# First-layer attention scores on tiles of the TensorE array, and half of the folded head weights on VectorE, in a graph-attention layer

## The chip, the cores and the metric

The kernel runs on one core of one Trainium2 (trn2) chip. The metric is device time of one execution in microseconds (us), as the median of the runs; every run also lists the granted clock of TensorE.

## The reference, cut to what matters

128 graphs of 64 nodes with 512 features pass through a layer norm and a ReLU, then a graph-attention layer with four heads, a second one with a single head, a feed-forward block, a second layer norm, and a residual addition. All is fp32.

```python
def _gat_heads(x, adj, W, a):
    Wh = einsum('bnf,hfo->bhno', x, W)
    f1 = einsum('bhno,ho->bhn', Wh, a[:, :O])
    f2 = einsum('bhno,ho->bhn', Wh, a[:, O:])
    e = f1[:, :, :, None] + f2[:, :, None, :]
    e = where(e > 0, e, 0.01 * e)
    e = where(adj > 0, e, NEG_INF)
    return einsum('bhnm,bhmo->bhno', softmax(e), Wh)

h   = relu(layernorm(x))                       # x: [128, 64, 512]
h   = elu(_gat_heads(h, adj, W_heads, a_heads)) # 4 heads of 512
out = elu(_gat_heads(h, adj, W_out, a_out))     # 1 head
ffn = relu(out @ w1 + b1) @ w2 + b2
x   = x + layernorm(ffn + out) * gamma + beta
```

## The kernel before

A tile holds 128 rows, which is two graphs. Four tiles make a group, so there are 16 groups.

**The scores.** f1 and f2 of the first layer come straight from the normalised input: the head weights W and the vectors a are folded once into `wa` (512 rows, 8 columns). f2 is needed along the free axis, so VectorE spreads it over a diagonal (`dg`) and TensorE multiplies by blocks of ones; f1 is added on VectorE.

```python
def project_f(p):                        # p: a pair of tiles
    pf = aux([P, 2, 2 * H], f"pf{p}")
    for j in range(2):
        hT = HT.pop(2 * p + j)
        for k in range(KC):
            nc.tensor.matmul(pf[:, j, :], hT[:, k, :], wa[:, k, :], ...)
    FF[p] = sm.tile([P, 2, 2, H], FP, ...)
    nc.vector.tensor_copy(FF[p], ...)
...
def softmax(f1, q, tag, t):
    dg = DG.pop(tag)
    pe = aux([P, q, N], f"{tag}pe{t}")
    nc.tensor.matmul(pe, blkones, dg, start=True, stop=True)
    nc.vector.tensor_tensor(e, pe, f1..., ALU.add)
    nc.vector.tensor_tensor(e, e, negm..., ALU.add)
    ...
```

**The products.** The large products are done in Strassen-Winograd form: seven products per matrix, one bank of PSUM each for products 1, 5 and 6; product 7 adds onto the bank of product 6 (`own[7] = 6`). VectorE must have read product 6 out (tile `t`) before product 7 may write there. With the order 1, 6, 5, 2, 7, 3, 4 it has the time of products 5 and 2 for that.

```python
own = {1: 1, 2: 1, 5: 5, 3: 5, 6: 6, 7: 6, 4: 6}
def after(p):
    if p in (1, 5, 6):
        nm = {1: "s1", 5: "s15", 6: "t"}[p]
        sb[nm] = wk.tile([P, 2, T], FP, tag=nm, ...)
        if p == 1:
            nc.scalar.copy(sb[nm], gb[1])
        else:
            nc.vector.tensor_tensor(sb[nm], gb[p], sb["s1"], ALU.add)
    ...
```

**The side list.** While TensorE does the steps of one large product, `run` asks for other work between them, evenly. Empty entries (`None`) only space the others out. Stage_a (scores and softmax of the group after next) has 15 entries; together with the feed-forward of the group before (`ff`), its transposes, the attention steps and the four finishing norms (`fin`) there are 45.

```python
def run(steps, side=()):
    side, done = list(side), 0
    for i, fn in enumerate(steps):
        fn()
        while done * len(steps) < (i + 1) * len(side):
            side[done]()
            done += 1

def stage_a(g):
    ...
    return [norms(p), norms(r), transposes(p), transposes(r),          # each a lambda
            f(p), None, attn_weights(p), f(r), None, attn_weights(r),
            None, transpose_weights(p), None, None, transpose_weights(r)]

# main loop, group g
tail = mix(ff, stage_a(g + 2))           # by place: (i + 0.5) / length
run(project2(g), mix(attn, tr) + tail + fin)
```

The next group's first products (tile `g_a`, `project1`) follow directly; beside them run `scores2`, eight multiply-accumulates on VectorE (tile `jf`).

## Time and profile before

| kernel before | value |
|---|---|
| median of 4 runs | 2445.72 us (2442.99 to 2447.22) |
| span of the profiled run | 2447.4 us |
| TensorE, VectorE, ScalarE, GpSimd busy | 97, 59, 31, 41% |
| period of one group | 144.96 us |

The prediction below shows the page's main lines. The list of waits of TensorE (us in total, times, longest) has for `g_a`:

```profile
PE g_a L240 <- issue: 5.3, 3, 3.2
```

One of the three, 1.45 us, is in the start. The other two stand before product 7, in the last two groups: 0.7 us and 3.2 us. In the last group VectorE's `t_a` ends only 10.1 us after the group's first product.

```profile
667.74 0.68 DVE L207 TENSOR_TENSOR t_a<-g_a,s_a 128x512 f32<-128x512 f32 x1
```

Four products take 670.80 - 663.90 = 6.90 us. The fifth in order, product 7, starts at once, because VectorE's `t_a` is over at 667.74 + 0.68 = 668.42, which is 4.5 us after the group's first product. TensorE needs it at 6.9 us, so the margin is 2.4 us.

### The profile page before, as it was taken

To read this page: it belongs to the slowest core of one execution; us is meant where nothing else is said; L and a number is where in the kernel's file an instruction comes from. 1 tells how busy PE (TensorE), PEld (TensorE's weight loads), DVE (VectorE), ACT (ScalarE), POOL (GpSimd) and SP (SyncE) were. 2 spreads that over 40 slices of the span, in tenths; PEclk is the share of its full clock that TensorE was granted. 3 is DMA by queue.
4 is the path that set the end of the run, shared out by engine and by line. 5 is a ranking of instruction groups with operands and counts; after the bars stand their busy time and mean duration, and the time that the engine had idled before them with its cause. 6 is when DMAs were issued, how large, how long until landed. Compare 5 with 4: busy or idle time off the path is not lost.

```text
span 2447.4 us, 32886 instructions
## 1 busy us (share of the span) xinstructions
PE 2382.2 (97%) x11745; PEld 2020.3 (83%) x11745; DVE 1446.5 (59%) x2515; ACT 770.9 (31%) x1353; POOL 1006.6 (41%) x848
## 2 busy tenths in 40 slices
PE   6799999999999999999999999999999999999996
PEld 6688888888888888888888888888888888878884
DVE  2655566474755748566574855657475574844536
ACT  1242514324152332414233251422415133231402
POOL 5733442534434344432534443253443435433323
PEclk6799999999999999999999999999999999999998
DMA  7644445454544545444454544545454454535442
GB/s 291 216 131 130 132 141 167 128 177 133 167 134 130 176 130 176 133 143 153 132 177 129 172 130 144 166 127 179 130 168 133 133 173 132 173 113 170 142 149 69
DMA packets 260481, 368.97 MB, mean 151 GB/s; under 512 B 22336, under 2 KB 145248, under 8 KB 260320
## 3 DMA queue, kind: packets, MB, share of 16 engines
q1 hardware_dynamic: 252160, 345.90, 44.2%
q10 hardware_dynamic: 5280, 10.49, 1.2%
q0 software_dynamic: 2880, 10.49, 1.1%
q8 instruction: 95, 1.56, 0.3%
q14 instruction: 66, 0.54, 0.1%
HBM read 339.53 MB, written 27.26 MB: 150 GB/s over the span
## 4 chain that ended last, share of the span: by engine, by line
PE 93%; DVE 3%; DMA 2%; issue 1%; POOL 1%; ACT 0%; SPq 0%; DVEq 0%; ACTq 0%; POOLq 0%
PE g_b L255 31%; PE g_a L240 31%; PE g_c L240 8%; PE g_d L255 7%; PE pz L453 4%; PE pf L314 2%; PE pa L585 2%; DMA x<-in_x_dram 1%; PE pzS L453 1%; PE pto L611 1%; PE s1pe L341 1%; PE pth L304 1%; PE s1pt L399 1%; PE pwa L147 1%; DVE o L658 0%
## 5 line engine op out<-in xcount | busy, mean ns | idle before, releaser
L255 PE MATMUL g_b<-w,h 128*128 128x256 f32 x2560 | 599.0, 380 | 0.0
L255 PEld LDWEIGHTS g_b<-w,h 128*128 128x128 f32 x2560 | 478.7, 190 | 74.6 <-issue 14.3
L240 PE MATMUL g_a<-zs_z,w 128*128 128x256 f32 x1536 | 357.9, 381 | 8.2 <-issue 5.3
L240 PE MATMUL g_a<-z,w 128*128 128x256 f32 x1536 | 363.0, 379 | 0.0
L240 PEld LDWEIGHTS g_a<-zs_z,w 128*128 128x128 f32 x1536 | 292.2, 191 | 57.3 <-issue 14.5
L240 PEld LDWEIGHTS g_a<-z,w 128*128 128x128 f32 x1536 | 291.6, 190 | 53.1 <-issue 15.2
L255 PE MATMUL g_b<-w,hS 128*128 128x256 f32 x1024 | 244.8, 385 | 0.0
L515 POOL TENSOR_TENSOR hS<-hS,h 128x512 f32<-128x512 f32 x64 | 81.4, 1272 | 385.0 <-DVE hS L477 384.4
L255 PEld LDWEIGHTS g_b<-w,hS 128*128 128x128 f32 x1024 | 189.5, 190 | 48.2 <-issue 13.0
L542 POOL TENSOR_TENSOR h<-h,h 128x512 f32<-128x512 f32 x64 | 84.2, 1315 | 286.0 <-PE g_b L255 285.9
L476 ACT ACTIVATE exc<-exc 128x512 f32<-128x512 f32 x256 | 161.0, 629 | 6.5
L265 POOL TENSOR_TENSOR zs_z<-zS,z 128x512 f32<-128x512 f32 x63 | 89.1, 1415 | 170.7 <-PE g_a L240 129.7
L477 DVE SCALAR_TENSOR_TENSOR h<-exc,h 128x512 f32<-128x512 f32 x128 | 104.5, 817 | 62.5 <-ACT exc L476 62.5
L542 POOL TENSOR_TENSOR h<-hS,h 128x512 f32<-128x512 f32 x64 | 81.3, 1271 | 138.6 <-PE g_b L255 138.5
L255 PE MATMUL g_d<-w,rt 128*128 128x256 f32 x512 | 122.2, 382 | 2.4 <-DVE n2ve L280 1.1
L267 POOL TENSOR_TENSOR zs_z<-z,zs_z 128x512 f32<-128x512 f32 x63 | 89.8, 1426 | 84.1 <-PE g_a L240 70.1
L475 ACT ACTIVATE exc<-h 128x512 f32<-128x512 f32 x128 | 80.6, 629 | 130.1 <-DVE h L512 130.1
L240 PE MATMUL g_c<-ot,w 128*128 128x256 f32 x512 | 121.0, 379 | 0.0
L240 PE MATMUL g_a<-zS,w 128*128 128x256 f32 x512 | 121.0, 379 | 0.0
L266 POOL TENSOR_TENSOR zs_z<-z,zs_z 128x512 f32<-128x512 f32 x63 | 80.6, 1280 | 80.5 <-PE g_d L255 63.7
L240 PEld LDWEIGHTS g_a<-zS,w 128*128 128x128 f32 x512 | 96.1, 190 | 18.8 <-issue 7.2
L255 PEld LDWEIGHTS g_d<-w,rt 128*128 128x128 f32 x512 | 96.0, 190 | 16.0 <-DVE n2ve L280 1.5
(145 smaller groups left out, 3754.9 us busy)
## 6 DMA issues: line engine op xcount, KB each, us to landing
w<-tc SPq DMA_DIRECT2D x640, 256.0 KB, 2.7
w<-in_L_gnn_W_heads_dram SPq DMA_DIRECT2D x192, 256.0 KB, 2.9
w<-in_L_gnn_W_out_dram SPq DMA_DIRECT2D x192, 256.0 KB, 2.8
w<-in_L_gnn_w_dram SPq DMA_DIRECT2D x96, 256.0 KB, 2.7
x<-in_x_dram SPq DMA_DIRECT2D x66, 256.0 KB, 4.0
xr<-in_x_dram SPq DMA_DIRECT2D x64, 256.0 KB, 2.8
out_dram<-o SPq DMA_DIRECT2D x64, 256.0 KB, 2.1
tc<-pt POOLq DMA_DIRECT2D x20, 512.0 KB, 4.8
```

The source lines that it names most:

```text
L240: nc.tensor.matmul(bk[:, o, :], w[:, k, ts(o, P)], a[:, k, :], start=start and o == 0 and k == 0, stop=k == 1, skip_group_check=True,)
L255: nc.tensor.matmul(bk[:, j, :], a[:, k, ts(j, P)], w[:, k, :], start=start and k == 0 and j == 0, stop=i == len(ms) - 1 and k == 1, skip_g ...
L265: eng.tensor_tensor(s2, s1, a11, ALU.subtract)
L266: eng.tensor_tensor(s4, a12, s2, ALU.subtract)
L267: eng.tensor_tensor(s3, a22, s2, ALU.subtract)
L314: nc.tensor.matmul(pf[:, j, :], hT[:, k, :], wa[:, k, :], start=(k == 0), stop=(k == KC - 1))
L453: nc.tensor.matmul(banks[b][:, c, :].rearrange("p (h n) -> p h n", h=H), src[rows, off + c * P:off + (c + 1) * P], at[rows, b], start=True ...
L475: nc.scalar.activation(ex, src, AF.Relu, scale=-1.0)
L476: nc.scalar.activation(ex, ex, AF.Exp, scale=-1.0)
L477: nc.vector.scalar_tensor_tensor(dst, ex, -1.0, src, ALU.add, ALU.max)
L515: nc.gpsimd.tensor_tensor(dst, dst, H1["22"][:, h], ALU.add)
L542: nc.gpsimd.tensor_tensor(dst[:, h], x0[:, h], x1[:, h], ALU.subtract)
```

## The change

The intent is to take 5.12 us per group of short TensorE work down by using parts of the array side by side, to start sooner, and to hide the last group's softmax.

- `project_f` computes f1 and f2 of four tiles transposed, with `wa` padded to 32 columns as the weight, on four column quarters of the array.
- The scores become a product of two factors: `L` holds f1 and ones, `R` holds ones and f2, and a sum over the small inner dimension gives f1 + f2. It runs on four quadrants.
- Two of the four heads are folded on VectorE, with no transposes on TensorE.
- The last group's softmax runs beside feed-forward steps.
- The weight ring shrinks from 12 to 11 buffers, and stage_a has another spacing.

```diff
-    ring = ctx.enter_context(tc.tile_pool(name="ring", bufs=12))
+    ring = ctx.enter_context(tc.tile_pool(name="ring", bufs=11))
...
-    wa = const.tile([P, KC, 2 * H], FP, name="wa")
+    wa = const.tile([P, KC, 32], FP, name="wa")
...
+    FH = 2
...
+    def fold_dve(m, ab):
+        for k in range(KC):
+            for c in range(2):
+                nc.vector.scalar_tensor_tensor(
+                    junk, MT[m][:, k, :], 1.0, ab[c], ALU.mult, ALU.mult,
+                    accum_out=wa[:, k, c * H + m:c * H + m + 1],
+                )
...
+    def project_f(g):
+        pf = aux([P, P], f"pf{g}")
+        for k in range(KC):
+            for j in range(G):
                 nc.tensor.matmul(
-                    pf[:, j, :], hT[:, k, :], wa[:, k, :], start=(k == 0), stop=(k == KC - 1)
+                    pf[32 * j:32 * j + 32], wa[:, k, :], HT[G * g + j][:, k, :],
+                    start=(k == 0), stop=(k == KC - 1), skip_group_check=True,
                 )
+        ...   # L: two ScalarE activations; U: VectorE; R: GpSimd (VectorE for group 0)
+    def scores1(g):
+        L, R = LR.pop(g)
+        pe = [aux([P, 2, H * N], f"s1pe{g}_{a}") for a in range(2)]
+        for q in range(2):
+            for a in range(2):
+                for b in range(NB):
+                    rows, cols = slice(64 * a, 64 * a + 64), slice(b * N, (b + 1) * N)
+                    nc.tensor.matmul(pe[a][cols, q, :]..., L[rows, q, cols], R[rows, :, cols], ...)
...
         return [
             lambda: norms(p), lambda: norms(r), lambda: transposes(p), lambda: transposes(r),
-            lambda: f(p), lambda: None, lambda: attn_weights(p), lambda: f(r), lambda: None,
-            lambda: attn_weights(r), lambda: None, lambda: transpose_weights(p), lambda: None,
-            lambda: None, lambda: transpose_weights(r),
-        ]
+        ] + wait + [lambda: project_f(g)] + wait * 2 + [
+            lambda: (scores1(g), attn_weights(p)), lambda: None, lambda: attn_weights(r),
+        ] + wait * 2 + [lambda: transpose_weights(p)] + wait * 2 + [lambda: transpose_weights(r)]
...
-            held = len(ff) - 7
-            run(project2(g), tr + [lambda: None] * 8 + ff[:held])
-            run(ff[held:] + fin, stage_e(g)[:15])
+            held = 2
+            run(project2(g), tr + [lambda: None] * 6 + ff[:held])
+            run(left, [scores2(g), ..., softmax2(g), ..., transpose_weights2(g), ..., attend2 x 4])
...
-    run(tr + ff[:12] + fin[:2] + ff[12:] + fin[2:])
+    run(tr + ff[:6] + last + ff[6:12] + fin[:2] + ff[12:] + fin[2:])
```

More of the change, by code (lines that the diff above doesn't have):

```diff
@@ L109, in gat_preln_kernel @@
     nc.vector.tensor_add(eye, ident[:, 0:N], ident[:, N:2 * N])
+    id32 = const.tile([P, 32], FP, name="id32")
+    nc.vector.tensor_reduce(id32, ident.rearrange("p (j r) -> p r j", r=32), AX.X, ALU.add)
+    headrow = const.tile([P, H], FP, name="headrow")
+    nc.vector.tensor_add(headrow, id32[:, 0:H], id32[:, H:2 * H])
+    isf = const.tile([P, 2], FP, name="isf")
+    nc.vector.tensor_reduce(isf, id32[:, 0:2 * H].rearrange("p (c h) -> p c h", c=2), AX.X, ALU.add)
+    isq = const.tile([P, 2, 2], FP, name="isq")
+    for q in range(2):
+        par = sm.tile([P, 1], FP, tag="par", name=f"par{q}")
+        nc.vector.tensor_reduce(
+            par, ident.rearrange("p (a q r) -> p q a r", a=2, q=2)[:, q], AX.XY, ALU.add
+        )
+        nc.vector.tensor_scalar(isq[:, q], isf, par, None, ALU.mult)
     mats = [W_heads[h] for h in range(H)]
@@ L117, in gat_preln_kernel @@
     MT, TC = {}, {}
-    wa = const.tile([P, KC, 2 * H], FP, name="wa")
+    wa = const.tile([P, KC, 32], FP, name="wa")
+    nc.vector.memset(wa, 0.0)
     def fetch(m):
@@ L122, in fetch @@
         nc.scalar.dma_start(out=MT[m], in_=mats[m].rearrange("(k p) o -> p k o", p=P))
+    FH = 2
     def load_a():
+        ar = wk.tile([2 * H, O], FP, tag="elu", name="ar", bufs=3)
+        nc.sync.dma_start(out=ar, in_=a_heads.rearrange("h (r p) -> (h r) p", p=O))
         rows = H * 2 * KC
@@ L128, in load_a, with spread_a, turn_a @@
         nc.sync.dma_start(out=ah, in_=a_heads.rearrange("h (r p) -> (h r) p", p=P))
+        return ar, ah
+    def spread_a(ar, m):
+        ab = []
+        for c in range(2):
+            pb = bank(f"pab{m}_{c}").rearrange("p a b -> p (a b)")
+            r = 2 * m + c
+            nc.tensor.matmul(
+                pb, ident[0:2 * H, r:r + 1].to_broadcast([2 * H, P]), ar, start=True, stop=True
+            )
+            ab.append(pb)
+        return ab
+    def turn_a(ah):
+        rows = H * 2 * KC
         pt = aux([P, rows], "pah")
@@ L131, in load_a, with fold_pe @@
         aT = const.tile([P, H, 2, KC], FP, name="aT")
-        nc.vector.tensor_copy(aT.rearrange("p h c o -> p (h c o)"), pt)
+        nc.scalar.copy(aT.rearrange("p h c o -> p (h c o)"), pt)
         return aT
-    def fold(m, aT, pw):
+    def fold_dve(m, ab):
+        for k in range(KC):
+            for c in range(2):
+                junk = wk.tile([P, O], FP, tag="t", name=f"jk{c}_{m}_{k}")
+                nc.vector.scalar_tensor_tensor(
+                    junk, MT[m][:, k, :], 1.0, ab[c], ALU.mult, ALU.mult,
+                    accum_out=wa[:, k, c * H + m:c * H + m + 1],
+                )
+    def fold_pe(m, aT, pw):
         for k in range(KC):
@@ L141, in fold @@
             wT = wk.tile([P, KC, P], FP, tag="elu", name=f"wT{m}_{k}", bufs=3)
-            if k % 2 == 0:
-                nc.scalar.copy(wT, pt)
-            else:
-                nc.vector.tensor_copy(wT, pt)
+            nc.scalar.copy(wT, pt)
             for o in range(KC):
                 nc.tensor.matmul(
-                    pw[:, k, :, m], wT[:, o, :], aT[:, m, :, o],
-                    start=(m == 0 and k == 0 and o == 0), stop=(o == KC - 1), skip_group_check=True,
+                    pw[:, k, :, m - FH], wT[:, o, :], aT[:, m, :, o],
+                    start=(m == FH and k == 0 and o == 0), stop=(o == KC - 1), skip_group_check=True,
                 )
@@ L295, in norm1 @@
             nc.gpsimd.tensor_tensor(HNS[t], HN[t][:, 0:T], HN[t][:, T:2 * T], ALU.add)
-    FF = {}
+    LR = {}
     HT = {}
@@ L306, in transpose_h @@
         nc.scalar.copy(HT[t], pt)
-    def project_f(p):
-        pf = aux([P, 2, 2 * H], f"pf{p}")
-        for j in range(2):
-            hT = HT.pop(2 * p + j)
-            for k in range(KC):
+    def project_f(g):
+        pf = aux([P, P], f"pf{g}")
+        for k in range(KC):
+            for j in range(G):
                 nc.tensor.matmul(
-                    pf[:, j, :], hT[:, k, :], wa[:, k, :], start=(k == 0), stop=(k == KC - 1)
-                )
-        FF[p] = sm.tile([P, 2, 2, H], FP, tag="f1", name=f"f1_{p}")
-        nc.vector.tensor_copy(FF[p], pf.rearrange("p t (c h) -> p c t h", c=2))
@@ L320, in gat_preln_kernel @@
-    DG = {}
-    def spread(f2, q, tag, t):
-        w = "s1" if q == 8 else "s2"
-        dg = sm.tile([P, q, N], FP, tag=w + "dg", name=f"{tag}dg{t}", bufs=1)
-        nc.vector.tensor_tensor(
-            dg,
-            eye[:, None, :].to_broadcast([P, q, N]),
-            f2[:, :, None].to_broadcast([P, q, N]),
+                    pf[32 * j:32 * j + 32], wa[:, k, :], HT[G * g + j][:, k, :],
+                    start=(k == 0), stop=(k == KC - 1), skip_group_check=True,
+                )
@@ new lines, in project_f @@
+        L = sm.tile([P, 2, P], FP, tag="L", name=f"L{g}", bufs=1)
+        for q in range(2):
+            nc.scalar.activation(L[:, q], pf, AF.Identity, bias=isq[:, q, 1:2], scale=isq[:, q, 0:1])
+        U = sm.tile([P, P], FP, tag="U", name=f"U{g}", bufs=1)
+        nc.vector.tensor_scalar(U, pf, isf[:, 1:2], isf[:, 0:1], ALU.mult, ALU.add)
+        R = sm.tile([P, H, P], FP, tag="R", name=f"R{g}", bufs=1)
+        eng = nc.vector if g == 0 else nc.gpsimd
+        eng.tensor_tensor(
+            R, U[:, None, :].to_broadcast([P, H, P]), headrow[:, :, None].to_broadcast([P, H, P]),
@@ L331, in spread @@
             ALU.mult,
         )
-        DG[tag] = dg
-    def softmax(f1, q, tag, t):
-        w = "s1" if q == 8 else "s2"
-        dg = DG.pop(tag)
-        pe = aux([P, q, N], f"{tag}pe{t}")
-        nc.tensor.matmul(
-            pe.rearrange("p h m -> p (h m)"), blkones.rearrange("p b n -> p (b n)"),
-            dg.rearrange("p h m -> p (h m)"), start=True, stop=True,
-        )
-        e = sm.tile([P, q, N], FP, tag=w + "e", name=f"{tag}e{t}", bufs=1)
-        nc.vector.tensor_tensor(e, pe, f1[:, :, None].to_broadcast([P, q, N]), ALU.add)
-        nc.vector.tensor_tensor(e, e, negm[:, None, :].to_broadcast([P, q, N]), ALU.add)
+        LR[g] = L, R
@@ new lines, in scores1 @@
+    def scores1(g):
+        L, R = LR.pop(g)
+        pe = [aux([P, 2, H * N], f"s1pe{g}_{a}") for a in range(2)]
+        for q in range(2):
+            for a in range(2):
+                for b in range(NB):
+                    rows, cols = slice(64 * a, 64 * a + 64), slice(b * N, (b + 1) * N)
+                    nc.tensor.matmul(
+                        pe[a][cols, q, :].rearrange("p (h m) -> p h m", h=H), L[rows, q, cols],
+                        R[rows, :, cols], start=(q == 0), stop=True, skip_group_check=True,
+                    )
+        for a in range(2):
+            E1[2 * g + a] = pe[a].rearrange("p t (h m) -> p (t h) m", m=N)
@@ L348, in softmax @@
+    def softmax(pe, f1, q, tag, t):
+        w = "s1" if q == 8 else "s2"
+        e = sm.tile([P, q, N], FP, tag=w + "e", name=f"{tag}e{t}", bufs=1)
+        mask = negm[:, None, :].to_broadcast([P, q, N])
+        if f1 is None:
+            nc.vector.tensor_tensor(e, pe, mask, ALU.add)
+        else:
+            nc.vector.tensor_tensor(e, pe, f1[:, :, None].to_broadcast([P, q, N]), ALU.add)
+            nc.vector.tensor_tensor(e, e, mask, ALU.add)
         nc.vector.scalar_tensor_tensor(e, e, ALPHA, e, ALU.mult, ALU.max)
@@ L380, in softmax @@
         return A
-    A1 = {}
-    def spread1(p):
-        spread(FF[p][:, 1].rearrange("p t h -> p (t h)"), 2 * H, "s1", p)
+    A1, E1 = {}, {}
     def attn_weights(p):
-        A1[p] = softmax(FF.pop(p)[:, 0].rearrange("p t h -> p (t h)"), 2 * H, "s1", p)
+        A1[p] = softmax(E1.pop(p), None, 2 * H, "s1", p)
     def transpose_weights(p):
@@ L422, in transposes @@
             transpose_h(2 * p + 1)
-        def f(p):
-            project_f(p)
-            spread1(p)
+        wait = [lambda: None]
         return [
             lambda: norms(p), lambda: norms(r), lambda: transposes(p), lambda: transposes(r),
-            lambda: f(p), lambda: None, lambda: attn_weights(p), lambda: f(r), lambda: None,
-            lambda: attn_weights(r), lambda: None, lambda: transpose_weights(p), lambda: None,
-            lambda: None, lambda: transpose_weights(r),
-        ]
+        ] + wait + [lambda: project_f(g)] + wait * 2 + [
+            lambda: (scores1(g), attn_weights(p)), lambda: None, lambda: attn_weights(r),
+        ] + wait * 2 + [lambda: transpose_weights(p)] + wait * 2 + [lambda: transpose_weights(r)]
     ZB = {}
@@ L568, in scores2 @@
                 )
-        F2[g] = f
-        spread(f[:, 1], G, "s2", g)
-    def softmax2(g):
-        A2[g] = softmax(F2.pop(g)[:, 0], G, "s2", g)
+        dg = sm.tile([P, G, N], FP, tag="s2dg", name=f"s2dg{g}", bufs=1)
+        nc.vector.tensor_tensor(
+            dg, eye[:, None, :].to_broadcast([P, G, N]), f[:, 1][:, :, None].to_broadcast([P, G, N]),
+            ALU.mult,
+        )
+        F2[g] = f, dg
+    def softmax2(g):
+        f, dg = F2.pop(g)
+        pe = aux([P, G, N], f"s2pe{g}")
+        nc.tensor.matmul(
+            pe.rearrange("p h m -> p (h m)"), blkones.rearrange("p b n -> p (b n)"),
+            dg.rearrange("p h m -> p (h m)"), start=True, stop=True,
+        )
+        A2[g] = softmax(pe, f[:, 0], G, "s2", g)
     def transpose_weights2(g):
@@ L586, in attend2 @@
         if j == 0:
-            OUT[g] = big.tile([P, G, FO], FP, tag="out", name=f"o{g}")
+            tag = "out" if g < NG - 1 else "z11"
+            OUT[g] = big.tile([P, G, FO], FP, tag=tag, name=f"o{g}")
         elu(OUT[g][:, j], pa, f"2_{g}_{j}")
@@ L671, in mix @@
         return [fn for _, _, fn in sorted(keyed, key=lambda k: k[:2])]
-    aT = load_a()
+    ar, ah = load_a()
     for m in range(H):
@@ L678, in gat_preln_kernel @@
         norm1(t)
+    ab = [spread_a(ar, m) for m in range(FH)]
+    aT = turn_a(ah)
     for t in range(G):
         transpose_h(t)
-    pw = aux([P, KC, 2, H], "pwa")
-    for m in range(H):
-        fold(m, aT, pw)
-    nc.vector.tensor_copy(wa.rearrange("p k (c h) -> p k c h", c=2), pw)
+    for m in range(FH):
+        fold_dve(m, ab[m])
+    pw = aux([P, KC, 2, H - FH], "pwa")
+    for m in range(FH, H):
+        fold_pe(m, aT, pw)
+    for c in range(2):
+        nc.vector.tensor_copy(wa[:, :, c * H + FH:(c + 1) * H], pw[:, :, c])
+    project_f(0)
+    scores1(0)
     for p in range(2):
-        project_f(p)
-        spread1(p)
         attn_weights(p)
@@ L731, in gat_preln_kernel @@
         else:
-            held = len(ff) - 7
-            run(project2(g), tr + [lambda: None] * 8 + ff[:held])
-            run(ff[held:] + fin, stage_e(g)[:15])
-    for fn in stage_e(NG - 1)[15:]:
-        fn()
+            held = 2
+            run(project2(g), tr + [lambda: None] * 6 + ff[:held])
+            left = ff[held:]
+            run(left, [
+                lambda: scores2(g), lambda: None, lambda: None, lambda: None, lambda: softmax2(g),
+                *[lambda: None] * 7, lambda: transpose_weights2(g), lambda: None,
+                *[lambda j=j: attend2(g, j) for j in range(G)], lambda: None,
+            ])
+    last = fin
     tr, ff, fin = feed_forward(NG - 1)
-    run(tr + ff[:12] + fin[:2] + ff[12:] + fin[2:])
+    run(tr + ff[:6] + last + ff[6:12] + fin[:2] + ff[12:] + fin[2:])
 _INS = [
```

## The prediction

> **What bounds the kernel now.** I read the page's list of engines first, then the 40 slices, then the chain that ended last.
>
> ```profile
> PE 2382.2 (97%) x11745; PEld 2020.3 (83%) x11745; DVE 1446.5 (59%) x2515; ACT 770.9 (31%) x1353; POOL 1006.6 (41%) x848
> PE   6799999999999999999999999999999999999996
> PEclk6799999999999999999999999999999999999998
> PE 93%; DVE 3%; DMA 2%; issue 1%; POOL 1%; ACT 0%; SPq 0%; DVEq 0%; ACTq 0%; POOLq 0%
> ```
>
> TensorE is busy for 97% of the span and carries 93% of the chain. Only the first two slices of 61 us and the last one show holes. So three places can give time: TensorE's own work in the middle, the start, and the end. Work on VectorE, ScalarE or GpSimd in the middle is hidden.
>
> Next the timeline of TensorE in the middle of one group of four tiles (columns: start us, us, engine, line, operation, tile, count).
>
> ```profile
> 574.96 1.89 PE L255 MATMUL g_b<-w,h 128*128 128x256 f32 x8
> 576.78 2.00 PE L453 MATMUL pz<-at,hn 64*128 64x256 f32 x16
> 578.71 1.99 PE L255 MATMUL g_b<-w,h 128*128 128x256 f32 x8
> ...
> 611.96 1.89 PE L255 MATMUL g_b<-w,h 128*128 128x256 f32 x8
> 613.69 1.85 PE L314 MATMUL pf<-wa,hT 128*128 128x8 f32 x16
> 615.39 1.97 PE L255 MATMUL g_b<-w,h 128*128 128x256 f32 x8
> ...
> 622.38 1.02 PE L341 MATMUL s1pe<-s1dg,blkones 128*128 128x512 f32 x2
> 623.24 1.89 PE L255 MATMUL g_b<-w,h 128*128 128x256 f32 x8
> ```
>
> I subtract starts, because the second column includes a pipeline tail that overlaps the next row. Eight g_b matmuls take 613.69 - 611.96 = 1.73 us, 0.216 us each for 256 columns. Sixteen pf matmuls of only 8 columns take 615.39 - 613.69 = 1.70 us, 0.106 us each: as much as 128 columns would, so the 128-column weight load (PEld) is what they pay for. Two s1pe matmuls of 512 columns take 0.86 us. Each occurs twice per group: 2 x 1.70 + 2 x 0.86 = **5.12 us per group**. In the source an fp32 product is one call; the trace counts two instructions for it (512 pf for 256 calls), and I count in those instructions.
>
> The same phase of g_a comes back every 144.95 us (starts 386.65, 531.61, 676.58), and no TensorE wait longer than a fraction of a microsecond lies in between. So a microsecond taken from TensorE there should be a microsecond saved, 15 times (the first group is in the start).
>
> The start, by stretches (per engine busy us and count; then PEclk, DMA share, GB/s), and two rows that fix its steps:
>
> ```profile
> 34.00:42.00 8.00, 6.00 (x30) 5.60 (x29) 1.88 (x3) 0.59 (x1) 5.65 (x7) 0.50 1.05 401
> 42.00:50.00 8.00, 8.00 (x41) 8.00 (x41) 1.70 (x3) 1.17 (x2) 5.48 (x7) 0.50 0.84 327
> 63.86 0.19 DVE L684 COPY wa<-pwa 128x32 f32<-128x32 f32 x1 [4.15 <-PE pwa L147]
> 100.71 1.99 PE L240 MATMUL g_a<-z,w 128*128 128x256 f32 x8
> ```
>
> The folded head weights (wa) are finished only at 63.9 us, at half the TensorE clock; the first Strassen product starts at 100.7 us.
>
> The end: the wait list gives TensorE 6.4 us before s2pt, waiting for VectorE's softmax of the last group.
>
> ```profile
> PE s2pt L579 <- DVE s2A L374: 6.4, 1, 6.4
> 2396.49 3.78 PE L585 MATMUL pa<-wh,at 128*128 128x512 f32 x4 [0.68 <-ACT at L581]
> ```
>
> After that idle stretch four pa take 3.78 us, some 0.86 us each, where the middle shows two in 0.86 us: the clock fell to half as well.
>
> **What the Trainium skill says.** (1) "TensorEngine Tiling (Array Packing)", Key Properties: tiles of the array load and multiply independently, but changing the tiling mode drains the engine. The trace agrees: sixteen pz, which use 64 rows each, take 578.71 - 576.78 = 1.93 us, against 16 x 0.216 = 3.46 us one after the other; half of 3.46 is 1.73, so two ran at once and about 0.20 us went to the switch. The g_b run behind it needs 1.83 us (to 580.54) instead of 1.73, another 0.10. I take **0.3 us per tiled run**. (2) "TensorE: Matmul & The Clock Gate", Part 3, gives 2.38 times for three column tiles and 10.6 for sixteen row-and-column tiles. No run so far shows column tiles, let alone in fp32; this is the step I am least sure of. (3) The same page, Part 1: an idle TensorE falls to half clock; the trace has 0.50 through the start and the slow pa at the end. (4) "VectorE: DVE Perf Modes" gives (N+151)/0.96 ns for an fp32 tensor operation, 691 ns at 512; the trace has 684 to 692 ns for such rows.
>
> **The change part by part.**
>
> *f1/f2 transposed (pf).* Removed: 32 instructions, 3.40 us per group. Added: 16 calls, 32 instructions of 128 moving columns, with wa padded to 32 columns as the weight, on four column quarters. One alone should take half of 0.216, so 0.108 us; all in a row 3.46 us; four at once 0.86 us. Plus 0.3 for the switch: 1.16 us. The weight load shrinks from 128 columns to 32 and should no longer bind.
>
> *Scores (s1pe).* Removed: 4 instructions of 512 columns, 1.72 us per group. Added: 8 calls, 16 instructions of 256 columns with 64 rows and 64 columns, on four quadrants: 16 x 0.216 = 3.46 in a row, 0.86 four at once, plus 0.3: 1.16 us. In the program the two instructions of one call are on the same tile, so four at once needs the engine to look past the waiting one. The pz pairs show that it does so for two tiles: otherwise half the calls would not have overlapped.
>
> So 5.12 becomes some 2.4 us with a little loss, 2.7 less, and 15 x 2.7 = **40 us**. If only two tiles overlap: 1.73 + 1.73 + 0.6 = 4.1, and 15 us. If none: 7.5, and 36 us lost.
>
> *Off the path in the middle.* VectorE loses 2 x (0.17 + 0.72 + 0.69) = 3.2 us per group (copy of f, s1dg, the f1 addition) and gains one 128-column operation; ScalarE gains two of 128 columns; GpSimd gains one 128x512 product (1.3 to 1.4 us in its rows). All three have room (busy 59, 31 and 41%). One weight buffer fewer (12 to 11) takes some 2 us of a lead of some 20 us; no TensorE wait for a weight DMA is listed. I give these nothing.
>
> *Start.* Half of the 16 fold steps leave TensorE. From 34 to 64 us the old kernel did 13 steps, 2.3 us each at half clock; eight less is 18 us. Against that, VectorE has 16 multiply-accumulates, about 0.75 + 0.08 us each by the jf rows (752 ns, and 79 ns for the accumulator read): 13.3 us, beside TensorE's 18. wa should be ready at about 46 us. The path behind it (products, scores, softmax, transposes) is a few us shorter too, but has a new chain of factor building. **20 us** in all.
>
> *End.* The last group's softmax now runs beside twelve of the feed-forward steps (1.73 us each, 21 us of TensorE work), so the 6.4 us wait and the half clock (eight pa x 0.43 = 3.4 us) should go. The normalisations of the group before move into the last feed-forward, where VectorE then has more to do (about 4 x 2.5 us). Net **8 us**.
>
> Sum: 40 + 20 + 8 = 68; 2445.4 - 68 = 2377. I say **2378 us**.
>
> **Rivals.** (a) Column quarters or quadrants do not overlap fully in fp32, because the moving streams or weight loads share a path. For: no column tile in the trace. Against: the pz pairs and the skill's figures. Two at once: 2378 + 25 = 2403. None: about 2445 to 2455, no gain. (b) A wait takes the place of the removed work: the scores now wait for a chain of three engines (ScalarE, VectorE, GpSimd) and GpSimd works in order, often held for g_b by write-after-read waits of 2 to 3 us. For: such waits stand in its timeline just at that point. Against: the new schedule leaves three steps, some 6 to 10 us, between projection and scores, where the chain needs about 0.35 + 0.3 + 1.4 us plus queueing. If it fails by 1 us per group: 2393. (c) The start is held by VectorE or by loads, not by the folds: with DMA share 1.0 until 42 us and VectorE waiting in order for x tiles, wa may come at 55 rather than 46: 2387.
>
> **Range and chances.** All right: 2365 to 2370. With (b) or (c) 2385 to 2395, with half of (a) 2400. Low 2352, high 2408. The 2% border is 2396.5, so the gain must exceed 49 us; the start and end alone (28 us) do not reach it. I put faster at 0.80, same at 0.17, slower at 0.03.
>
> **What would show each step.** Between rows of TensorE's timeline, the pf run should take about 1.2 us instead of 2 x 1.70, the scores run about 1.2 instead of 2 x 0.86; the period of g_a should fall from 144.95 to about 142.2 us with no new TensorE wait on R or L; wa should be written near 46 us and the first g_a start near 78; the wait before s2pt should be gone, and pa there should run at full clock. The prediction is wrong above all if tiles run one at a time.

## More of the kernel before

The timelines of TensorE and VectorE at a usual turn (start us, us, engine, line, operation, tile, shape, count):

```profile
663.90 1.89 PE L240 MATMUL g_a<-z,w 128*128 128x256 f32 x8
...
670.80 3.62 PE L240 MATMUL g_a<-zs_z,w 128*128 128x256 f32 x16
```

## The result, and the profile after

The changed kernel takes **2434.4 us** (median of 4 runs, 2432.96 to 2437.24) against 2445.72. The ratio of the two is 0.9956 with a 95% interval of 0.9939 to 0.9974, which at the 2% border is "same". Ratios here are the mean time of one kernel's fast runs over that of the other's of the same rounds, so they are not quite the ratio of the medians. The time lies 26 us above the predicted range.

The page's line of engines and TensorE's list of waits after the change:

```profile
PE 2344.2 (96%) x11849; PEld 1961.4 (81%) x11849; DVE 1451.6 (60%) x2468; ACT 787.1 (32%) x1386; POOL 1020.0 (42%) x863
```

```profile
PE g_a L284 <- issue: 31.5, 14, 3.5
...
PE s2pt L636 <- DVE s2A L427: 0.3, 1, 0.3
```

TensorE's busy time fell by 38.0 us where the span fell by only 14.6. `g_a` now waits before product 7 in 14 groups, 31.5 us in all. The wait before `s2pt` went from 6.4 to 0.3 us, as meant.

**The tiled runs.** TensorE's timeline around them:

```profile
458.48 1.08 PE L358 MATMUL pf<-hT,wa 128*32 128x128 f32 x32
459.50 1.99 PE L299 MATMUL g_b<-w,h 128*128 128x256 f32 x8
461.32 1.89 PE L284 MATMUL g_c<-zs_o,w 128*128 128x256 f32 x8
...
468.32 1.09 PE L383 MATMUL s1pe<-R,L 64*64 64x256 f32 x16
469.35 1.99 PE L299 MATMUL g_d<-w,rt 128*128 128x256 f32 x8
471.18 1.89 PE L299 MATMUL g_b<-w,hS 128*128 128x256 f32 x8
```

By differences of starts, `pf` takes 459.50 - 458.48 = 1.02 us and `s1pe` 1.03 us. The eight matmuls before and behind each of them take some 0.09 us longer than their usual 1.73 us. That is about 1.20 us for each run, 2.40 for both, where 5.12 stood before.

**The new wait.** The first products of the group's next turn, on TensorE and VectorE:

```profile
646.90 1.89 PE L284 MATMUL g_a<-z,w 128*128 128x256 f32 x8
...
652.08 1.89 PE L284 MATMUL g_a<-z,w 128*128 128x256 f32 x8
655.89 5.38 PE L284 MATMUL g_a<-zs_z,w 128*128 128x256 f32 x16 [1.93 <-issue]
661.11 1.89 PE L284 MATMUL g_a<-z,w 128*128 128x256 f32 x8
```

```profile
650.65 0.68 DVE L596 TENSOR_TENSOR wh<-g_b,s_b 128x512 f32<-128x512 f32 x1
...
655.11 0.68 DVE L251 TENSOR_TENSOR t_a<-g_a,s_a 128x512 f32<-128x512 f32 x1
```

Product 2 is issued from 652.08 and would be through at 652.08 + 1.73 = 653.81. Product 7 starts at 655.89, **2.1 us** late. The profile names no releaser ("issue"), but VectorE's `t_a`, which product 7 must wait for, ends at 655.79, 0.10 us before. The same 0.10 us stands in the other turns that I looked at (`t_a` over at 511.18, product 7 at 511.28; 802.13 and 802.24). `t_a` now ends 8.9 us after the group's first product instead of 4.5, and TensorE needs it at 6.9. Between the two VectorE rows stand four `jf`, one statistic of the next norm and `s2dg`, nearly without a gap: the chain is late as a whole.

The wait has a second cost. The sixteen matmuls behind it take 661.11 - 655.89 = 5.22 us instead of 3.45. Two stretches of 3.41 us (busy us and count of PE, PEld, DVE, ACT, POOL; then PEclk, DMA share, GB/s):

```profile
652.91:656.32 3.41, 1.49 (x7) 1.01 (x7) 3.38 (x12) 1.23 (x2) 0.00 (x0) 1.00 0.99 302
656.32:659.73 3.41, 3.41 (x10) 2.66 (x9) 2.44 (x6) 0.00 (x0) 0.34 (x1) 0.50 0.38 139
```

In the first VectorE is busy for 3.38 of 3.41 us, while TensorE, by its modelled ends, is busy for 1.49. In the second the granted clock is 0.50: 7 or 8 matmuls take about 0.43 us each. That happens behind 11 of the 14 waits and costs about 1.7 us each time.

Which waits it follows can be read from the trace. In this one, between 300 and 2300 us, the half clock always comes in single pieces of 3.41 us, and their starts are whole multiples of that length apart (803.09 - 656.32 = 146.77, which is 43 of them). I cut this part of the run into such windows and counted TensorE as idle from 0.216 us after its last start to its next one. Each of the 11 waits puts at least 2.09 us of idle TensorE into one window, and the next window has half clock. The other three lie across a border, with at most 1.87 us on either side (the one at 1092.76 to 1095.08 is 2.3 us long), and nothing follows. In the traces of e1, e2, e3, e7 and e8 the line falls at the same place, for waits over 1 us: 91 windows at full clock hold up to 1.98 us of them, and the clock stays full; 41 hold 1.99 us or more, and the next window has half clock.

**The accounts.** The chain of waits holds the same 72 `g_a` instructions of every group; the first and the last of them before and after (start us, us, engine, tile, line, count) split the span into start, middle and end:

```profile
241.20 15.54 PE g_a L240 x72
...
2271.05 15.54 PE g_a L240 x72
```

```profile
225.84 15.54 PE g_a L284 x72
...
2267.82 15.54 PE g_a L284 x72
```

| part | before, us | after, us | change, us | predicted, us |
|---|---|---|---|---|
| to the first of these | 241.20 | 225.84 | -15.4 | -20 |
| 14 periods between | 2029.85 | 2041.98 | **+12.1** | **-38** (14 x 2.7) |
| from the last on | 176.35 | 164.98 | -11.4 | -8 |
| span | 2447.4 | 2432.8 | -14.6 | |

The prediction's fifteenth 2.7 us falls outside these 14 periods. The miss is in the middle: a period mostly lasts 146.3 us where the half clock follows the wait, and 144.6 where it does not; before it lasted 144.96.

**The start.** On VectorE, GpSimd and TensorE:

```profile
48.16 0.24 DVE L747 COPY wa<-pwa 128x8 f32<-128x8 f32 x2 [12.68 <-PE pwa L191]
...
88.61 4.36 DVE L310 TENSOR_TENSOR zs_z<-z,zs_z 128x512 f32<-128x512 f32 x1
```

```profile
88.71 1.28 POOL L202 TENSOR_TENSOR pt<-pw 128x512 f32<-128x512 f32 x1
```

```profile
81.27 1.99 PE L284 MATMUL g_a<-z,w 128*128 128x256 f32 x8
...
98.20 3.78 PE L284 MATMUL g_a<-zs_z,w 128*128 128x256 f32 x8 [7.85 <-DVE t_a L251]
```

`wa` is there at 48.2 us instead of 63.9, and the first product at 81.3 instead of 100.7. But 7.85 us of that gain are then lost, again to `t_a`: a VectorE sum that takes about 0.7 us elsewhere takes 4.36 us beside three weight sums of GpSimd from 88.71 to 92.4, and `t_a` (97.45 to 98.14) stands behind it.

### The profile page after: what moved, and what is told of

It reads as the page before. It is cut to its first block, busy times and chain, and to the rows that moved or that the text cites. A ratio compares the mean times of both kernels' runs of the same rounds, so it can differ in the third digit from the quotient of the medians.

```text
span 2432.8 us, 33084 instructions
## 1 busy us (share of the span) xinstructions
PE 2344.2 (96%) x11849; PEld 1961.4 (81%) x11849; DVE 1451.6 (60%) x2468; ACT 787.1 (32%) x1386; POOL 1020.0 (42%) x863
## 4 chain that ended last, share of the span: by engine, by line
PE 92%; DVE 2%; issue 2%; POOL 2%; DMA 2%; ACT 0%; SPq 0%; DVEq 0%; POOLq 0%; ACTq 0%
PE g_b L299 32%; PE g_a L284 32%; PE g_c L284 8%; PE g_d L299 8%; PE pz L499 4%; PE pa L642 2%; PE pzS L499 1%; PE pto L669 1%; PE pth L348 1%; PE s1pt L449 1%; DMA pw<-in_L_gnn_W_out_dram 1%; PE s1pe L383 1%; PE pf L358 1%; DMA pw<-in_L_gnn_w_dram 0%; DMA aj<-in_adj_dram 0%
## 5 line engine op out<-in xcount | busy, mean ns | idle before, releaser
L284 PE MATMUL g_a<-zs_z,w 128*128 128x256 f32 x1536 | 376.7, 395 | 41.4 <-issue 31.5
L284 PEld LDWEIGHTS g_a<-zs_z,w 128*128 128x128 f32 x1536 | 304.0, 199 | 98.7 <-issue 43.9
```

What stands on the lines that cost most here:

```text
L284: nc.tensor.matmul(bk[:, o, :], w[:, k, ts(o, P)], a[:, k, :], start=start and o == 0 and k == 0, stop=k == 1, skip_group_check=True,)
```

## The experiments

My theory after the comparison: TensorE's saving is real; VectorE's chain at the end of a group is behind, and product 7 waits for its last member. At first I put that down to the later softmaxes (theory A); after e1 to e4, to the new spacing of the side work as a whole (theory A2). Rivals: the smaller weight ring; the place of the softmaxes; the new factors themselves; a start or an end that gives nothing. In the short diffs of stage_a the lambdas are left out. The runs were made on two chips (e5 to e8 on the second), each beside the kernel before on the same chip, with medians of 2443.69 to 2447.03 us. For a few us the difference of two ratios says more than that of two medians; each ratio is known to some 4 us.

| run | median us (lowest to highest) | ratio to before, 95% interval |
|---|---|---|
| e1 softmaxes earlier, 17 entries | 2480.22 (2475.97 to 2483.8) | 1.0144 (1.0124 to 1.0164) |
| e2 score sums moved | 2417.5 (2415.1 to 2420.66) | 0.9889 (0.9871 to 0.9907) |
| e3 kernel before, 17 entries | 2494.55 (2494.02 to 2495.81) | 1.0204 (1.0188 to 1.0221) |
| e4 kernel before, 11 buffers | 2444.85 | 1.001 (0.9983 to 1.0037) |
| e5 changed kernel, 15 entries | 2386.13 (2383.66 to 2386.3) | 0.975 (0.9735 to 0.9765) |
| e6 half of the score sums | 2386.93 | 0.9756 (0.9742 to 0.9771) |
| e7 old end | 2445.02 | 0.9997 (0.998 to 1.0014) |
| e8 old folding | 2444.59 | 0.9992 (0.9977 to 1.0007) |
| e9 filled wait | 2416.49 | 0.9881 (0.9862 to 0.99) |
| e10 e5 with later weight sums | 2382.4 (2381.41 to 2384.18) | 0.9746 (0.973 to 0.9761) |

### e1: the softmaxes earlier, the list as long

```diff
-        ] + wait + [project_f] + wait*2 + [(scores1, attn p), None, attn r]
-        + wait*2 + [tw p] + wait*2 + [tw r]
+        ] + [project_f] + wait + [(scores1, attn p), None, attn r]
+        + wait*2 + [tw p] + wait*3 + [tw r] + wait
```

> The changed kernel with one thing moved: in the side list of a group the joint projection stands one slot earlier and the scores with the first softmax two slots earlier (same length, same arithmetic). Theory A (VectorE is late: the joint projection pushed both softmaxes some 10 us later, into a stretch where VectorE has no room, so that t_a of head 0 comes about 2.1 us too late for the product that reuses its PSUM bank, and the clock then falls to half for seven matmuls): the wait shrinks to under 0.5 us in most groups, the slow matmuls go, the period of a group falls from 146.2 to about 142.5 us, the time to about 2385 us. Theory B (the wait is for weights, because of the 11 buffers, or for GpSimd's sums with its extra product R): nothing of theirs is moved, the wait stays near 2.1 us and the time near 2434 us.

It took 2480.22 us, 46 us more than the changed kernel, where theory A had expected some 50 less. The wait before product 7 was only a little shorter (1.6 to 1.7 us), and `t_a` still ended 8.4 us or more after the group's first product. A second wait came, 14 times and 43.2 us in all: TensorE's `g_d`, in the feed-forward, waited for `zs_r`, a block sum of VectorE.

```profile
633.11 3.36 PE L299 MATMUL g_d<-w,zs_r 128*128 128x256 f32 x8 [3.25 <-issue]
```

The run before it starts at 627.96, so 633.11 - 627.96 = 5.15 us pass for a run of 1.73; 3.4 us are lost, and the eight matmuls behind take 636.26 - 633.11 = 3.15 us, most of them at half clock. The place of the softmaxes alone is therefore not the cause of the first wait, and a step of side work moved on VectorE can make a wait elsewhere. The period was about 150.0 us.

### e2: the second layer's score sums moved

```diff
-            [scores2] + gap * 6 + [softmax2] + gap * 6
+            gap * 3 + [scores2] + gap * 5 + [softmax2] + gap * 4
```

> The changed kernel with the eight score sums of the second layer (jf, VectorE, 0.76 us each) emitted three slots later in the next group, so that t_a of head 0 can go before them on VectorE; nothing is taken away. Theory A: t_a comes 2 to 3 us sooner after the first products, the 2.1 us wait and the seven slow matmuls go, time about 2385 to 2395 us, unless the softmax of the second layer then comes late in its turn. Theory B: no change, about 2434 us.

It took 2417.5 us, 17 us less, but it did not test what it was meant to: the built program still had the `jf` ahead of `t_a` on VectorE. `t_a` ended at +8.6 to +8.8 us in most groups, and the wait was mostly 1.75 to 2.0 us. What changed is that the half clock mostly did not follow, as these waits leave less than 2 us of idle time in a window; the period was then 144.3 to 144.6 us. About the order of `jf` and `t_a` it is inconclusive.

### e3: only the spacing, in the kernel before

```diff
-            f(p), None, attn_weights(p), f(r), None, attn_weights(r), None, ...
+            None, None, f(p), None, attn_weights(p), f(r), None, attn_weights(r), None, ...
```

> The kernel before, whose arithmetic is untouched, with its two pairwise projections, scores and softmaxes delayed by two slots, to the slots where the changed kernel has its softmaxes. Theory A: the wait before the second product on the bank of t_a, and half-clock matmuls behind it, appear in the kernel before too; its period rises from 145.0 to 147 to 149 us and its time to 2475 to 2505 us. Theory B: no wait, period 145.0, time 2445 us as before.

Two empty entries, and no other change, made the kernel before some 2% slower: 2494.55 us (the interval of the ratio lies across the border of 2%). TensorE's and VectorE's timelines at the same place:

```profile
529.93 1.89 PE L240 MATMUL g_a<-z,w 128*128 128x256 f32 x8
533.75 3.48 PE L240 MATMUL g_a<-zs_z,w 128*128 128x256 f32 x15 [1.92 <-issue]
```

```profile
532.97 0.68 DVE L207 TENSOR_TENSOR t_a<-g_a,s_a 128x512 f32<-128x512 f32 x1
```

It is the wait of the changed kernel: `t_a` ends at 533.65, product 7 starts at 533.75, 2.1 us late. The list shows 33.0 us in 15 waits of `g_a`, 14 of them this one. The period is 147.5 us, or 149.3 to 149.6 where the half clock follows. The wait needs nothing of the new arithmetic. This run delays the softmaxes and lengthens the list at once, so it cannot tell the two apart; e1, with early softmaxes and a long list, does.

### e4: only the smaller ring, in the kernel before

```diff
-    ring = ctx.enter_context(tc.tile_pool(name="ring", bufs=12))
+    ring = ctx.enter_context(tc.tile_pool(name="ring", bufs=11))
```

> The kernel before with 11 weight buffers in place of 12, nothing else. Theory A: no TensorE wait appears, 2445 us (same within 0.3%). Theory B in its form of late weights: a wait of about 2 us per group appears in front of g_a, period about 147 to 148.7 us, time 2475 to 2500 us.

2444.85 us, ratio 1.001: the ring costs nothing that can be seen. The opposite test, the changed kernel with 12 buffers, could not be run: it does not build, because the pool of small tiles then needs 13.1 KB per partition and 11.2 are left.

### e5: the changed kernel with the old spacing

```diff
-        ] + wait + [project_f] + wait*2 + [(scores1, attn p), None, attn r]
-        + wait*2 + [tw p] + wait*2 + [tw r]
+        ] + [project_f] + wait + [(scores1, attn p), None, None, attn r]
+        + wait + [tw p] + wait*2 + [tw r]
```

> The changed kernel with the side list of a group brought back from 17 to the 15 slots of the kernel before: joint projection in slot 4 (where the first pairwise one stood), scores and first softmax in 6, second softmax in 9, transposes in 11 and 14. Theory A2 (formed after the first four runs: the two added empty slots push the last feed-forward steps and the four closing normalisations later against the next group, VectorE ends them at +3.8 us after the first product in place of -0.3, and t_a comes at +8.9 in place of +4.5, where TensorE needs it at about +6.9): t_a is back at about +4.5 to +5.5 us, no wait, no half clock, period about 142.3 us (145.0 less 2.7), time 2380 to 2392 us. Theory A (early softmax is what matters) was weakened by e1; it would give the same here only by chance. Rival C (the new scores and their chain of three engines cost the time by themselves, at whatever slot): a wait stays, period over 145, time over 2420 us.

2386.13 us, 48 us less than the changed kernel and 2.5% under the kernel before; the outputs are right. The turn on TensorE and VectorE:

```profile
507.48 3.62 PE L284 MATMUL g_a<-zs_z,w 128*128 128x256 f32 x16
```

```profile
504.41 0.68 DVE L251 TENSOR_TENSOR t_a<-g_a,s_a 128x512 f32<-128x512 f32 x1
```

`t_a` ends at 505.09, 4.5 us after the group's first product (500.57), exactly as in the kernel before, and product 7 does not wait (507.48 - 500.57 = 6.91). The period is 142.1 us, 2.85 under the kernel before; the prediction had 2.7. With e3 this makes a square of two changes:

| | 15 entries | 17 entries | difference |
|---|---|---|---|
| old scores | 2445.7 | 2494.6 | +49 |
| new scores, fold and end | 2386.1 | 2434.4 | +48 |
| difference | -60 | -60 | |

The two lists of 17 are not the same entry for entry, but the two effects add. The new work is worth 60 us either way, and the spacing takes 48 of them.

### e6: half of the score sums taken away

```diff
-            for c in range(2):
+            for c in range(1):
...
+        nc.vector.tensor_copy(f[:, 1], f[:, 0])
```

> The changed kernel with 17 slots, but the second half of the layer-2 score sums (four jf per group, 3 us of VectorE just ahead of t_a) taken away and the first half copied in their place; the result is wrong on purpose. Theory A2: the wait is VectorE work, so t_a comes about 2.5 to 3 us sooner, at about +6, the wait of 2.1 us goes to under 0.3 us and the slow matmuls with it; period about 142.5, time about 2390 us. Rival D (TensorE waits there for something else that ends with t_a by chance: weights or GpSimd sums): wait unchanged, about 2430 us.

This kernel is wrong on purpose (relative error 0.131). With four of a group's eight `jf` gone, `t_a` ended at +6.1 to +7.4 us, in most groups ahead of the 6.9 us at which TensorE needs it (five still waited, 0.2 to 0.6 us), no half clock followed there, and the time was 2386.93 us, as e5. The spacing was that of the changed kernel. So the wait hangs on how much VectorE has queued ahead of `t_a`, not on the list in itself.

### e7: the old end

```diff
-            held = 2
-            run(project2(g), tr + [lambda: None] * 6 + ff[:held])
...
+            held = len(ff) - 7
+            run(project2(g), tr + [lambda: None] * 8 + ff[:held])
+            run(ff[held:] + fin, stage_e(g)[:15])
...
-    run(tr + ff[:6] + last + ff[6:12] + fin[:2] + ff[12:] + fin[2:])
+    run(tr + ff[:12] + fin[:2] + ff[12:] + fin[2:])
```

> The changed kernel with its end (the order of the last group, and the buffer of its output tile) put back as before. By the traces the end from the last layer-2 scores on took less: 14.6 us less in all at the last instruction against 3.2 at the last group's first product, so 11 us. Expected: 11 us more, about 2445 us; if the end gave nothing, 2434.

The last output tile goes back to its old buffer too. 2445.02 us: the new end is worth 10.6 us by the medians, and 10.0 by the ratios (0.9997 - 0.9956 of 2446). The wait before `s2pt` is back, at 6.6 us.

### e8: the old folding

```diff
-    FH = 2
+    FH = 0
...
```

> The changed kernel with all four heads folded on TensorE as before (copies alternating between ScalarE and VectorE). In the changed trace wa was ready at 48.2 us in place of 63.9 and the first product started at 81.3 in place of 100.7, but 8 us were lost again at 98 us, where VectorE and GpSimd were behind. Expected: wa near 64 us, first product near 98 us, a wait of 1 to 3 us in place of the 8, so 10 to 16 us more: 2444 to 2450 us. If VectorE and GpSimd set the start whatever the folds do: 2434 to 2438.

All four heads fold on TensorE again (with the copies taking turns on two engines, as before). 2444.59 us: folding half on VectorE is worth 10.2 us by the medians, 8.8 by the ratios. `wa` came at 62.7 us (48.2 with the new folding) and the first `g_a` product at 93.1 (81.3), so the folding brings that forward by 11.8 us. Instead of the expected 1 to 3 us TensorE waited 7.0 us here too, before product 6 at 102.05 us: not for `t_a`, but for VectorE's sum `zs_z`, which ends at 101.94.

### e9: the wait filled with useless work

```diff
+        def fill():
+            if g >= 2 and h == 0:
+                pj = aux([P, KC, P], f"junk{g}")
+                for i in range(18):
+                    nc.tensor.transpose(pj[:, i % KC, :], ident, ident)
...
+            lambda: (fill(), s[4]()),            # ahead of product 7
```

> The changed kernel with 18 useless transposes of the identity (0.11 us each, 2.0 us) put on TensorE in each group exactly where it waits for t_a, so that the wait is filled and not idle. If the half clock behind the wait is caused by the idle stretch (clock theory), the seven slow matmuls go although nothing useful was done: period from 146.3 to about 144.4 to 144.7 us, time from 2434 to about 2410 to 2418 us. If the slow matmuls have another cause (operands not there, a shared port), nothing is gained, 2434 us or more.

TensorE does 18 transposes of the identity while it would wait. Nothing useful is added, yet the kernel takes 2416.49 us, 18 us less.

```profile
508.76 2.13 PE L569 MATMUL junk<-ident 128*128 128x128 f32 x18
510.99 3.69 PE L284 MATMUL g_a<-zs_z,w 128*128 128x256 f32 x16
```

Product 7 starts as late as before, 2.2 us behind product 2, but at full clock. By differences of starts, no `g_a` matmul after 200 us takes over 400 ns (76 do in the changed kernel), and the period is mostly 144.6 to 145.0 us. So about 18 of the 48 us are the half clock behind the wait. The other 30 are mostly the wait, 31.5 us in the list.

### e10: e5, and two weight sums asked for later

```diff
-    for m in range(len(mats)):
+    for m in range(2 * H):
...
+        if g == 0:
+            for m in (M1, M2):
+                fetch(m)
+                weight_sums(m)
```

> The 15-slot version of e5 with the block sums of w1 and w2 (eight GpSimd products and their loads, first needed in group 1) asked for after the first layer of group 0 in place of before it, to take GpSimd out of VectorE's way at 88 to 98 us, where TensorE waits 7.8 us for t_a. The scheduler has kept the four sums of w1 at nearly their old place, so only half may move. If GpSimd's sums are what holds VectorE there: the wait falls by 3 to 6 us, time 2380 to 2384 us. If not: 2386 us as in e5.

This was meant to remove the 7.85 us wait of the start by moving GpSimd's sums for w1 and w2 behind it. 2382.4 us and a ratio of 0.9746 against e5's 0.975: by the ratios the two can't be told apart. The wait for `t_a` at 98 us went, but others came, one of 2.2 us at about 86 us and one of 4.3 us at about 96 us, where TensorE waits for ScalarE's copy `s_a`. e5 and e10 beat both kernels.

## Why the prediction was wrong, point by point

- **The tiled runs: right.** Predicted 1.16 us for each, measured 1.20; 5.12 became 2.40 us per group as forecast, so rival (a), tiles that do not overlap, did not happen. In e5, where nothing hides it, the period fell by 2.85 us.
- **The step that failed** is the one that gives VectorE's share nothing: "All three have room (busy 59, 31 and 41%)" and, with it, "a microsecond taken from TensorE there should be a microsecond saved". 59% is the mean over a group. At the end of a group VectorE is full, and `t_a` had a margin of only 2.4 us before TensorE would wait. The kernel before already showed it in its last group, where that margin was used up and TensorE waited 3.2 us; the prediction looked at three groups in the middle. The diff shows two more empty entries in stage_a's list; I read its new positions only as slack for the factors and did not ask what else the list spaces out. The traces show what it moved at the end of a group, and it is what the list's arithmetic gives: one feed-forward product, the third from the last, starts 14.69 us before the group's first `g_a` product in the changed kernel (646.90 - 632.21), and so it does in e1 and e3, where the kernel before (663.90 - 647.48) and e5 (642.67 - 626.25) have 16.42. The two products behind it stay where they were. The first finishing norms, which need that product, begin 1.73 us later, and the last one ended 3.8 us after the group's first product instead of 0.3 before it. The other part of that delay lies in the norms themselves. VectorE's row for their last step, before and after (count, busy us, mean ns, then the waits before it in us):

```profile
L658 DVE SCALAR_TENSOR_TENSOR o<-o,n2rs,xr 128x512 f32<-128x512 f32 x64 | 49.2, 804 | 6.2 <-POOL n2rs L282 6.0
```

```profile
L716 DVE SCALAR_TENSOR_TENSOR o<-o,n2rs,xr 128x512 f32<-128x512 f32 x64 | 76.2, 1193 | 14.1 <-POOL n2rs L326 14.1
```

With four such rows in a group, 1193 instead of 804 ns (794 in e5) is 1.6 us, and the waits for GpSimd's `n2rs` grew from 6.2 to 14.1 us in all. In the turn at 646.90 two such rows took 1.67 and 1.75 us, each beside a GpSimd sum. That this one step of the list starts the whole delay is read from the traces and not tested: no run moves that entry alone.

- **Size of the failure.** The middle was to give 38 us and took 12, a miss of 50 us. e5 gives 39 us there (its chain has these products from 228.70 to 2219.12, 1990.4 us). The difference is a wait of mostly 2.1 to 2.4 us, the half clock behind it in most groups, and about 0.4 us more per group that I did not place.
- **Rival (b)** had the right form, a wait in place of the work removed, but the wrong place: it looked at R and L ahead of the scores. There is no such wait in the middle.
- **The start: right in mechanism, a little large.** `wa` came at 48 us (46 predicted) and the first product at 81.3 (78). That is 19.4 us sooner, but the gain to the first common point was 15.4 us, not 20: a wait of 7.85 us followed at 98 us, where the kernel before lost 2.8 in two waits. A wait of 7.0 us for another VectorE result stands in e8, so VectorE is late there without the new folding too. By e8 the folding gives 9 to 10 of the 15.4 us; what gives the rest was not tested. Rival (c) did not come true for `wa`, but VectorE did hold the start later on.
- **The end: right, a little small.** 10 to 11 us by e7 and 11.4 by the accounts, against 8.
- **The ring: right.** e4 shows no cost.

## What to carry to other kernels

Before counting a saving on the bounding engine in full, find the operations of other engines that it waits for in program order, and read how long before the need each of them ends; that margin, not the mean busy share, says what room there is. Empty entries in a software schedule are a change of their own: work out beside which step every other entry lands, and build the new work with the old spacing as well. A wait of 2.1 us on TensorE cost 3.8 us where half clock followed it, and whether it followed hung on where the wait lay in the clock's windows.

## What the Trainium skill lacked or had wrong

- "TensorE: Matmul & The Clock Gate", Part 1, ties the idle clock to at least one idle window of about 3.4 us. Here windows of that length show (pieces of half clock of 3.41 us, whole multiples of it apart), but about 2.0 us of idle TensorE inside one window was enough: nine waits of 2.1 to 2.45 us and two of 3.4 and 3.7 us brought half clock for 7 or 8 matmuls each, and filling the wait with 18 small transposes removed it and 18 us.
- "TensorEngine Tiling (Array Packing)", Key Properties, says that switching the mode drains the engine, but gives no size. Around each tiled run the neighbours took some 0.09 us more on each side. It also has no fp32 figure for column quarters: 32 instructions of 128 columns took 1.02 us, where one after the other at 0.108 us would be 3.46.
- "SBUF — State Buffer", Who interferes with whom, says that a VectorE instruction with two SBUF inputs contends with a GpSimd instruction that reads SBUF, and that the loser blocks. The trace agrees, and adds how long it can last behind several of them: 4.36 us for one sum beside three GpSimd sums of 1.27 us.
